# An adaLN block on one core: the FFN's modulation made as columns, and the first FFN input turned by VectorE and DMAs

## The chip, the cores and the metric

The kernel runs on one core of one Trainium2 chip. The metric is the device time of one execution in microseconds (us), the median over several runs. The engines are TensorE (PE, with its weight loads listed apart as PEld), VectorE (DVE), ScalarE (ACT) and GpSimd (POOL); SyncE (SP) issues most of the DMAs, ScalarE's queue a few.

## The reference

One transformer block with adaptive layer norm, batch B = 8, S = 1024 rows, D = 256, FFN width 1024, all in f32.

```python
mod = (silu(c) @ wmod).reshape(8, 6, 1, 256)          # c: 8x256, wmod: 256x1536
sa, ca, ga, sb, cb, gb = mod[:, 0..5]
ga = (2 * (ga >= 0) - 1) * maximum(abs(ga), 0.25)     # gb likewise
h = layernorm(x) * (1 + ca) + sa
scores = (h * w_lhs) @ (h * w_rhs).T                  # 1024 x 1024 per batch element
x = x + ga * (softmax(scores) @ h)
h = layernorm(x) * (1 + cb) + sb
x = x + gb * (relu(h @ W1 + b1) @ W2 + b2)
```

The six parts of mod are, in order, shift, scale and gate of the attention (0, 1, 2) and of the FFN (3, 4, 5).

## The kernel before

The batch elements b are worked through one after the other, in eight steps i of 128 rows each. A half g of a batch element is 512 rows, four tiles of 128. The FFN of batch element b - 1 (and of the first half of b) is done between the attention steps of b. The order of instructions on each engine is written out by hand: the last statement, `pin`, ties every instruction to the one before it on its engine, so an engine that waits holds up all that stands behind it. The same holds for the queue of SP.

**The scores** form a symmetric matrix (the two weightings meet in one product over d). For each tile of rows i `direct(b, i)` (L412) computes only from column tile i on, into PSUM tiles psc, and ScalarE copies them to sc. The rest of the column comes by mirroring: for b = 0 `mirror_first` turns 128x128 blocks on TensorE (ptm) and ScalarE copies them; for b > 0 `mirror` has VectorE turn 32x32 blocks (Tm, L435), and `move` writes them to DRAM in four DMAs (D_m, L306) and reads them back in another order in one (L309). `row_max(b, i)` (L463) takes the maximum of row tile i over all columns, and so needs the mirrors of the tiles before it. `max_turn` (pm, L468) turns the maximum on TensorE, `subtract` (L475) writes scores minus maximum to pT, `exponent` (L484) applies the exponential, and `product` (po, L501) multiplies by xg on TensorE. `product_out` (L513 and L515) divides, adds to x, and takes the statistics for the FFN's norm.

**Inputs of the FFN.** For half g, `ffn_rstd` makes the reciprocal deviation on ScalarE, `ffn_norm` the normalised rows xn in a tile X, `ffn_blocks` turns xn in 32x32 blocks on VectorE (T_f, L322) and sends it through DRAM with `move` (D_f, X_f), and `ffn_turn` applies the modulation modT into hT, VectorE for the first half of the columns and ScalarE for the other; POOL then makes the sums hs from hT. The first input, (0, 0), goes another way: its normalisation is on VectorE (L663) in step i = 6, and `ffn_turn`, in step i = 7, turns it with eight transposes on TensorE into PSUM (ptx, L695). `pair_products` (L726) of batch 1, step 0, is the first user of hT and hs.

**The modulation.** `mod_rows(part, parts)` (L194) computes parts of mod with the 8 batch elements on the partitions: scT, the silu of c, is the weight (8 columns) and up to 512 columns of wmod stream past; ScalarE copies the result to `mod`. `mod_columns(part)` (L210) turns two parts with four transposes so that d lies on the partitions. At the start mod_rows(0, 2) is made, then, once the second piece of wmod (wm) has landed, mod_rows(2, 1) and mod_rows(5, 1), just ahead of the first `direct`. VectorE then makes both gates at once and writes four rows for each batch element to rows_sb: two for the attention and two, gate and gate times b2, for the FFN. They go to DRAM as rows_d; `load_rows` reads the first two back for every batch element, and `load_last` the other two for the last one. mod_rows(3, 2) comes between mirror(0, 1) and max_turn(0, 1). In step i = 0 of batch 0, `make_columns` turns the two FFN rows into gcol (pt_g, L1031) and parts 3 and 4 into modT (pmc, L210, and L1073, L1074).

Of the kernel before, what the change touches and what calls it, by code (L numbers as in the profile page):

```python
# [17 lines left out]
P = 128  # L18
# [6 lines left out]
def adaln_block_kernel(  # L25
# [69 lines left out]
    c_sb, b2_row = early_d[:B, 0], early_d[:B, 1]  # L95
    wv, b1_rows = early_d[: 2 * ND, 2, 0:P], early_d[:NI, 3, 0:P]
# [18 lines left out]
    )  # L115
    load_x0(2, nc.sync)
# [3 lines left out]
    nc.sync.dma_start(out=b2_row, in_=b2.partition_broadcast(B))  # L120
# [9 lines left out]
    zeros, sign = early_a[:, 0], early_a[:B, 1].rearrange("b (j d) -> b j d", d=D)  # L130
    nc.vector.memset(zeros, 0.0)
    early_c = two.tile([P, 4, D], F32, tag="hT", name="early_c", bufs=1)
    rows_sb = early_c[:B]
# [39 lines left out]
    cols = const.tile([P, NI + 2 * ND], F32, name="cols")  # L173
# [7 lines left out]
    b1_col = lambda i: cols[:, i : i + 1]  # L181
    w_cols = lambda side: cols[:, ds(NI + side * ND, ND)].rearrange(
# [4 lines left out]
    mod, gate = early_b[:B, 0:6], early_b[:B, 6:8]  # L187
# [26 lines left out]


# [19 lines left out]
    def load_rows(b, queue=nc.scalar):  # L235
        queue.dma_start(out=rows_tile(b), in_=rows_d[b][0:2, :].partition_broadcast(P))
# [411 lines left out]
    def ffn_norm(b, g):  # L648
        mv, r = ffn.pop(("r", g))

        X = two.tile([P, NV, NT * V], F32, tag="X", name=f"X_f{b}_{g}", bufs=1)
        xn = X.rearrange("p a m -> p (a m)").rearrange("p (j d) -> p j d", d=D)
        if b + g > 0:
            shift = work.tile([P, TH], F32, tag="rs", name=f"rs_f{b}_{g}")
            nc.vector.scalar_tensor_tensor(shift, mv[:, :, 0], -1.0, r, ALU.mult, ALU.mult)
        for j in range(TH):
            if b + g > 0:
                nc.scalar.activation(
                    xn[:, j, :], x_t[b, g][:, j, :], AF.Identity,
                    scale=r[:, j : j + 1], bias=shift[:, j : j + 1],  # L660
                )
                continue
            nc.vector.tensor_scalar(  # L663
                xn[:, j, :], x_t[b, g][:, j, :], mv[:, j, 0:1], r[:, j : j + 1],
                ALU.subtract, ALU.mult,
            )
        ffn["xn", g] = xn, X
# [13 lines left out]
    def ffn_blocks(b, g):  # L681
        if (b, g) == (0, 0):
            return
        xn, X = ffn.pop(("xn", g))
        ffn["X", g] = turn_blocks(lambda k: xn[:, :, ts(k, P)], f"f{b}_{g}", X)

    def ffn_turn(b, g):
        hT = two.tile([P, ND, HALF], F32, tag="hT", name=f"hT_{b}_{g}", bufs=1)
        split = lambda T: T.rearrange("p (t a v) -> p t a v", a=NV, v=V)
        if (b, g) == (0, 0):  # L690
            xn, X = ffn.pop(("xn", g))[0], []
            for k in range(ND):
                pt = ps_t.tile([P, HALF], F32, tag="t", name=f"ptx_{b}_{g}_{k}")
                for t in range(TH):
                    nc.tensor.transpose(pt[:, ts(t, P)], xn[:, t, ts(k, P)], ident)  # L695
                X.append(split(pt))
        else:
            X = ffn.pop(("X", g))
            X = [X[:, k] for k in range(ND)]
        for k in range(ND):  # L700
            rows = split(hT[:, k, :])
            shift = modT[:, 0, k, b : b + 1]
            scale = modT[:, 1, k, b : b + 1]
            if k % 2 == 0:
                nc.vector.tensor_scalar(rows, X[k], scale, shift, ALU.mult, ALU.add)
            else:
                nc.scalar.activation(rows, X[k], AF.Identity, bias=shift, scale=scale)


        hs = two.tile([P, 3, H2], F32, tag="hs", name=f"hs_{b}_{g}", bufs=1)  # L710
        b11, b12 = hT[:, 0, 0:H2], hT[:, 0, H2:HALF]
        b21, b22 = hT[:, 1, 0:H2], hT[:, 1, H2:HALF]
        add = nc.gpsimd.tensor_tensor
        add(hs[:, 0], b12, b11, ALU.subtract)
        add(hs[:, 2], b22, b12, ALU.subtract)
        add(hs[:, 1], b22, hs[:, 0], ALU.subtract)
        add(b12, b21, hs[:, 1], ALU.subtract)
        ffn["hT", g] = hT, hs
# [170 lines left out]
    def load_last():  # L889
        last_ = two.tile([P, NT, NV, NT, V], F32, tag="sc", name="w2g", bufs=1)  # L890
        last_ = last_.rearrange("p i a j v -> p (i a j v)")
        w2g = last_[:, 0 : NI * D].rearrange("p (i d) -> p i d", d=D)
        rows = last_[:, NI * D : (NI + 2) * D].rearrange("p (j d) -> p j d", d=D)
        nc.sync.dma_start(out=w2g, in_=W2.rearrange("(k p) d -> p k d", p=P))
        nc.sync.dma_start(out=rows, in_=rows_d[B - 1][2:4, :].partition_broadcast(P))
        ffn["w2g"], ffn["grows"] = w2g, rows
        for i in range(NI):
            later(w2g[:, i, :], w2g[:, i, :], rows[:, 0, :], ALU.mult)
# [66 lines left out]
    def sum_weights():  # L965
# [16 lines left out]
    mod_rows(5, 1)  # L982
# [3 lines left out]


    raw = mod[:, 2:6:3, :]
    nc.vector.tensor_scalar(sign, raw, 0.0, 2.0, ALU.is_ge, ALU.mult)
    nc.vector.scalar_tensor_tensor(gate, raw, -1.0, raw, ALU.mult, ALU.max)  # L990
    nc.vector.tensor_scalar(gate, gate, GATE_MIN, None, ALU.max)
    nc.vector.scalar_tensor_tensor(gate, sign, -1.0, gate, ALU.add, ALU.mult)

    nc.vector.scalar_tensor_tensor(
        rows_sb[:, 0, :], mod[:, 1, :], 1.0, gate[:, 0, :], ALU.add, ALU.mult
    )
    nc.vector.tensor_tensor(rows_sb[:, 1, :], mod[:, 0, :], gate[:, 0, :], ALU.mult)
    nc.vector.tensor_copy(rows_sb[:, 2, :], gate[:, 1, :])
    nc.vector.tensor_tensor(rows_sb[:, 3, :], gate[:, 1, :], b2_row, ALU.mult)
# [5 lines left out]
    rows_d = dram.tile([B, 4, D], F32, name="rows_d")  # L1005
# [18 lines left out]

    gcol = const.tile([P, 2, ND, B], F32, name="gcol")

    def make_gcol():
        pg = ps_a.tile([P, HALF], F32, tag="a", name="pt_g")
        for j in range(2):
            for k in range(ND):  # L1030
                nc.tensor.transpose(  # L1031
                    pg[:, ts(j * ND + k, B)], rows_sb[:, 2 + j, ts(k, P)], ident[:B, :B]
                )
        nc.scalar.copy(gcol.rearrange("p j k b -> p (j k b)"), pg[:, : 2 * ND * B])
# [24 lines left out]
    mod_rows(3, 2)  # L1059
# [8 lines left out]
    def make_columns():  # L1068
        make_gcol()
        columns(b1_rows, 0)  # L1070
        nc.gpsimd.tensor_tensor(b1_step, cols[:, NH:NI], cols[:, 0:NH], ALU.subtract)
        pmb = mod_columns(3)
        nc.vector.tensor_copy(modT[:, 0], pmb[:, 0])  # L1073
        nc.vector.tensor_scalar(modT[:, 1], pmb[:, 1], 1.0, None, ALU.add)  # L1074

    def early(b, i):

        if b == 0:
# [3 lines left out]
            elif i == 5:  # L1082
                ffn_rstd(0, 0)
# [5 lines left out]
            elif i == 5:  # L1089
                prepare_turn(1, 0)  # L1090
            elif i == 6:
# [7 lines left out]
    def turns(b, i):  # L1099
# [6 lines left out]
        elif b == 0 and i == 3:  # L1106
            prepare_blocks(1, 1)
# [12 lines left out]
    def norms(b, i):  # L1120
# [18 lines left out]
        if i == 6:  # L1139
            if b == 0:  # L1140
                ffn_norm(b, 0)
# [8 lines left out]
    for b in range(B):  # L1150
        for i in range(NT):
# [8 lines left out]
            if (b, i) == (0, NT - 2):  # L1160

                prepare_turn(1, 1)
                product(b, i)
# [3 lines left out]
                mirror(*ahead)  # L1167
                early(b, i)
# [283 lines left out]
```

## Time and profile before

| | |
|---|---|
| time, median of 3 runs | 757.05 us (756.62 to 757.45) |
| the profiled execution, its own time | 756.93 us |
| its span in the trace | 755.1 us |
| PE busy | 749.1 us |
| PEld / DVE / ACT / POOL busy | 623.4 / 574.9 / 374.9 / 570.9 us |
| granted TensorE clock | full in all 40 slices |
| traffic with HBM | 50.62 MB read, 43.81 MB written |

Times in the profile are us from the start of the span. A row of the timeline has start and length of a group of like instructions, engine, line, operation, output<-input, and in brackets the idle time before it with what ended it. An f32 product on TensorE leaves two records, a transpose one. A row of the chain has start, length, engine, tile, line and the number of records. "SPq" rows are the issues of DMAs, not their transfers.

### The profile page before, as it was taken

The page shows a single profiled execution, that of the slowest core. Times are in us where ns is not written, and L with a number is a line of the kernel's source. Part 1 is how long each engine was busy: PE and PEld are TensorE (multiplying, and loading weights), DVE is VectorE, ACT ScalarE, POOL GpSimd, SP SyncE. Part 2 cuts the span into 40 slices and gives each one's busy share as a digit, 9 for nine tenths or more (in the row PEclk, how much of TensorE's full clock was granted, in tenths as well). Part 3 has the DMA queues.
Part 4 walks back from the last instruction along what each step waited for, and adds up shares of the span by engine and source line. Part 5 has one row for each costly group of instructions (what it writes and reads, how often), then busy time and mean ns, then how long its engine had stood idle before and what let it go on. Part 6 is the DMA issues. An engine that isn't in the chain of part 4 may idle for free.

```text
span 755.1 us, 11883 instructions
## 1 busy us (share of the span) xinstructions
PE 749.1 (99%) x3876; PEld 623.4 (83%) x3876; DVE 574.9 (76%) x1259; ACT 374.9 (50%) x688; POOL 570.9 (76%) x658
## 2 busy tenths in 40 slices
PE   8999999999999999999999999999999999999998
PEld 4686889788897888888888878988889788888887
DVE  7787879778796879968878688876889777685632
ACT  4554646635375454745546444563546535252521
POOL 3762796878968798788877699777996888669741
PEclk9999999999999999999999999999999999999999
DMA  9033442455443453445534555245553354133220
GB/s 308 16 112 98 131 133 74 135 178 152 127 120 123 153 153 110 147 118 158 164 99 119 153 154 161 74 127 172 155 152 85 119 166 133 50 91 126 84 85 28
DMA packets 106213, 95.21 MB, mean 126 GB/s; under 512 B 29700, under 2 KB 98848, under 8 KB 106152
## 3 DMA queue, kind: packets, MB, share of 16 engines
q1 hardware_dynamic: 98408, 85.81, 38.6%
q10 hardware_dynamic: 7744, 8.65, 3.7%
q8 instruction: 30, 0.49, 0.3%
q14 instruction: 31, 0.25, 0.1%
HBM read 50.62 MB, written 43.81 MB: 125 GB/s over the span
## 4 chain that ended last, share of the span: by engine, by line
PE 96%; DMA 1%; DVE 1%; ACT 1%; issue 0%
PE psc L412 16%; PE pa L726 11%; PE po L501 10%; PE pr L593 7%; PE pb L726 7%; PE pc L726 7%; PE yc L806 6%; PE ya L806 6%; PE yb L806 6%; PE pq L593 5%; PE pp L549 5%; PE py L916 4%; PE yd L806 3%; DMA wm<-in_L_wmod_dram 1%; PE pm L468 1%; PE pmr L194 0%
## 5 line engine op out<-in xcount | busy, mean ns | idle before, releaser
L412 PE MATMUL psc<-rT,lT 128*128 128x512 f32 (+3 forms) x384 | 134.8, 487 | 0.0
L780 POOL TENSOR_TENSOR f<-f,kept 128x512 f32<-128x512 f32 x64 | 81.5, 1274 | 42.8 <-DVE f L779 20.1
L419 ACT COPY sc<-psc 128x512 f32<-128x512 f32 (+3 forms) x96 | 44.7, 476 | 119.9 <-PE psc L412 113.0
L484 ACT ACTIVATE pT<-pT 128x1024 f32<-128x1024 f32 x64 | 67.6, 1056 | 70.6 <-DVE pT L475 70.5
L475 DVE TENSOR_TENSOR pT<-sc,pm 128x1024 f32<-128x1024 f32 x64 | 77.3, 1208 | 29.3 <-PE pm L468 13.7
L412 PEld LDWEIGHTS psc<-rT,lT 128*128 128x128 f32 x384 | 66.4, 191 | 37.2 <-issue 25.6
L501 PE MATMUL po<-xg,pT 128*128 128x257 f32 x352 | 80.6, 380 | 0.0
L463 DVE TENSOR_REDUCE m<-sc 128x1 f32<-128x1024 f32 x64 | 77.4, 1209 | 2.2 <-ACT sc L419 1.8
L501 PEld LDWEIGHTS po<-xg,pT 128*128 128x128 f32 x352 | 66.2, 190 | 10.0 <-issue 0.7
L747 ACT COPY kept<-pa 128x512 f32<-128x512 f32 x64 | 37.4, 584 | 69.3 <-PE pa L726 69.1
L726 PE MATMUL pb<-hs,w1s 128*128 128x256 f32 x256 | 65.9, 380 | 0.1
L726 PE MATMUL pc<-hT,w 128*128 128x256 f32 x256 | 65.7, 379 | 0.0
L880 POOL TENSOR_TENSOR x<-x,Y 128x512 f32<-128x512 f32 x28 | 35.1, 1276 | 29.3 <-DMA Y<-D_y 29.3
L789 ACT ACTIVATE f<-f 128x512 f32<-128x512 f32 x64 | 39.8, 622 | 34.7 <-POOL f L780 34.7
L642 POOL TENSOR_TENSOR x<-x,rows 128x256 f32<-128x256 f32 x64 | 44.8, 732 | 13.8 <-ACT rows L1022 10.6
L726 PEld LDWEIGHTS pb<-hs,w1s 128*128 128x128 f32 x256 | 48.5, 190 | 7.3 <-DVE f L765 0.8
L726 PEld LDWEIGHTS pc<-hT,w 128*128 128x128 f32 x256 | 48.6, 190 | 6.7
L806 PE MATMUL yc<-f,w2s 128*128 128x256 f32 x224 | 51.3, 379 | 0.0
L435 DVE STREAM_TRANSPOSE Tm<-sc 128x896 f32<-128x896 f32 (+6 forms) x49 | 34.3, 701 | 20.3 <-ACT sc L419 19.6
L806 PEld LDWEIGHTS yc<-f,w2s 128*128 128x128 f32 x224 | 41.5, 190 | 8.1 <-issue 2.9
L549 PEld LDWEIGHTS pp<-xg,pT 128*128 128x128 f32 x336 | 41.9, 192 | 5.1 <-DVE st_b L241 1.4
L799 POOL TENSOR_TENSOR ft<-f 128x256 f32<-128x256 f32 x56 | 40.8, 729 | 6.8 <-ACT f L790 6.8
(166 smaller groups left out, 1821.1 us busy)
## 6 DMA issues: line engine op xcount, KB each, us to landing
D_f<-T_f SPq DMA_DIRECT2D x60, 128.0 KB, 2.5
X_f<-D_f SPq DMA_DIRECT2D x15, 512.0 KB, 3.7
D_a<-T_a SPq DMA_DIRECT2D x56, 128.0 KB, 2.8
D_y<-T_y SPq DMA_DIRECT2D x56, 128.0 KB, 2.9
Y<-D_y SPq DMA_DIRECT2D x14, 512.0 KB, 3.4
out_dram<-x SPq DMA_DIRECT2D x14, 512.0 KB, 4.4
X_a<-D_a SPq DMA_DIRECT2D x13, 512.0 KB, 3.4
x<-in_L_attn_x_dram ACTq DMA_DIRECT2D x12, 512.0 KB, 3.4
```

The lines of the kernel that those rows point to most:

```text
L412: nc.tensor.matmul(psc[:, : hi - lo], lhsT=lT_t[b, i // TH][:, k, ts(i % TH, P)], rhs=rT_t[b, n][:, k, lo - n * HALF : HALF], start=(k == ...
L419: nc.scalar.copy(score_row(b, i)[:, lo // V : hi // V, :], psc[:, : hi - lo].rearrange("p (n v) -> p n v", v=V),)
L463: nc.vector.tensor_reduce(m, score_row(b, i), AX.XY, ALU.max)
L475: nc.vector.tensor_tensor(pT.rearrange("p j (a v) -> p j a v", v=V), score_columns(b, i), pm[:, :P].rearrange("p (j a v) -> p j a v", j=1, ...
L484: nc.scalar.activation(pT_t[b, i], pT_t[b, i], AF.Exp)
L501: nc.tensor.matmul(po[:, : D + 1], lhsT=pT[:, t, :], rhs=xg_t[b][:, t, 0 : D + 1], start=(t == 0), stop=(t == NT - 1),)
L549: nc.tensor.matmul(out, lhsT=lhs[:, t, :], rhs=xg_t[b][:, h * TH + t, P : P + XS], start=(t == 0), stop=(t == TH - 1),)
L593: nc.tensor.matmul(out, lhsT=lhs[:, t, :], rhs=rhs[:, t, :], start=(t == 0), stop=(t == TH - 1),)
L642: queue.append(lambda: nc.gpsimd.tensor_tensor(out, in0, row, op))
L726: nc.tensor.matmul(out, lhsT=lhsT, rhs=rhs, start=True, stop=True)
L780: nc.gpsimd.tensor_tensor(f[:, c::NH, hi], f[:, c::NH, hi], kept[:, None, hi].to_broadcast([P, 2, H2]), ALU.add,)
L806: nc.tensor.matmul(out, lhsT=lhs(c), rhs=rhs(c), start=(c == 0), stop=(c == NH - 1))
```

## The change

Parts 3, 4 and 5 of mod are no longer made as rows. A new function `mod_direct` takes 128x128 pieces of wmod as the weights and the 8 columns of scT as the moving operand: twelve products, whose result (128 partitions, 3 parts x 2 halves x 8 batch elements) ScalarE copies to mod_ffn. It stands where mod_rows(3, 2) stood; mod_rows(5, 1) and both sets of transposes in make_columns go. The FFN's gate, its product with b2 and modT are made from mod_ffn on VectorE (the four steps of the gate are now the function `make_gate`) in `keep_columns`, in step i = 6 of batch 0. b2 is loaded as two rows beside w_lhs and w_rhs, ahead of the second half of x's first element and of the second piece of wmod, and turned with them. rows_d keeps the two attention rows; for the last batch element two small DMAs write gcol's columns to last_d, from which load_last reads.

The first FFN input now goes like the others: `ffn_rstd(0, 0)` moves from step 5 to step 4, `ffn_norm(0, 0)` is on ScalarE in step 5 behind prepare_turn(1, 0), and `ffn_blocks(0, 0)` turns it on VectorE in step 6, behind prepare_turn(1, 1) and ahead of product(0, 6), and sends it through DRAM. The second half of batch 1's attention input, which held the tile X until now, gets the tile ft.

```diff
-    c_sb, b2_row = early_d[:B, 0], early_d[:B, 1]
-    wv, b1_rows = early_d[: 2 * ND, 2, 0:P], early_d[:NI, 3, 0:P]
+    c_sb = early_d[:B, 0]
+    wv, b1_rows = early_d[: 3 * ND, 2, 0:P], early_d[:NI, 3, 0:P]
...
+    nc.sync.dma_start(out=wv[2 * ND : 3 * ND, :], in_=b2.rearrange("(k p) -> k p", p=P))
     load_x0(2, nc.sync)
     load_x0(3, nc.sync)
     nc.sync.dma_start(out=wm[:, :, 2 * D : 6 * D], in_=wmod_v[:, :, 2 * D : 6 * D])
     nc.sync.dma_start(out=b1_rows, in_=b1.rearrange("(k p) -> k p", p=P))
-    nc.sync.dma_start(out=b2_row, in_=b2.partition_broadcast(B))
...
-    mod, gate = early_b[:B, 0:6], early_b[:B, 6:8]
+    mod, gate = early_b[:B, 0:3], early_b[:B, 6]
+    mod_ffn = early_c[:, 2, 0 : 3 * ND * B].rearrange("p (n k b) -> p n k b", n=3, k=ND)
+    MB = early_c[:, 3, 0 : 2 * ND * B].rearrange("p (n k b) -> p n k b", n=2, k=ND)
...
+    def mod_direct():
+        pc = ps_a.tile([P, HALF], F32, tag="a", name="pmd")
+        for n in range(3):
+            for h in range(ND):
+                for k in range(ND):
+                    nc.tensor.matmul(
+                        pc[:, ts(n * ND + h, B)],
+                        lhsT=wm[:, k, ds((3 + n) * D + h * P, P)],
+                        rhs=scT[:, k, :],
+                        start=(k == 0),
+                        stop=(k == ND - 1),
+                    )
+        nc.scalar.copy(
+            mod_ffn.rearrange("p n k b -> p (n k b)"), pc[:, : 3 * ND * B]
+        )
...
 def ffn_norm(b, g):
-        if b + g > 0:
-            shift = work.tile([P, TH], F32, tag="rs", name=f"rs_f{b}_{g}")
-            nc.vector.scalar_tensor_tensor(shift, mv[:, :, 0], -1.0, r, ALU.mult, ALU.mult)
+        shift = work.tile([P, TH], F32, tag="rs", name=f"rs_f{b}_{g}")
+        nc.vector.scalar_tensor_tensor(shift, mv[:, :, 0], -1.0, r, ALU.mult, ALU.mult)
         for j in range(TH):
-            if b + g > 0:
-                nc.scalar.activation(
...
-            nc.vector.tensor_scalar(
-                xn[:, j, :], x_t[b, g][:, j, :], mv[:, j, 0:1], r[:, j : j + 1],
-                ALU.subtract, ALU.mult,
+            nc.scalar.activation(
+                xn[:, j, :], x_t[b, g][:, j, :], AF.Identity,
+                scale=r[:, j : j + 1], bias=shift[:, j : j + 1],
             )
...
 def ffn_turn(b, g):
-        if (b, g) == (0, 0):
-            xn, X = ffn.pop(("xn", g))[0], []
-            for k in range(ND):
-                pt = ps_t.tile([P, HALF], F32, tag="t", name=f"ptx_{b}_{g}_{k}")
-                for t in range(TH):
-                    nc.tensor.transpose(pt[:, ts(t, P)], xn[:, t, ts(k, P)], ident)
-                X.append(split(pt))
...
+        X = ffn.pop(("X", g))
+        X = [X[:, k] for k in range(ND)]
...
     mod_rows(2, 1)
-    mod_rows(5, 1)
     direct(0, 0, range(1))
...
+    make_gate(gate, mod[:, 2, :], gate, sign)
...
-    rows_d = dram.tile([B, 4, D], F32, name="rows_d")
+    rows_d = dram.tile([B, 2, D], F32, name="rows_d")
...
     def make_gcol():
-        pg = ps_a.tile([P, HALF], F32, tag="a", name="pt_g")
-...
+        make_gate(gcol[:, 0], mod_ffn[:, 2], MB[:, 0], MB[:, 1])
+        nc.vector.tensor_tensor(gcol[:, 1], gcol[:, 0], w_cols(2), ALU.mult)
         for j in range(2):
+            nc.sync.dma_start(
+                out=last_d[j].rearrange("(k p) -> p k", p=P), in_=gcol[:, j, :, B - 1]
+            )
...
     exponent(0, 0)
-    mod_rows(3, 2)
+    mod_direct()
     max_turn(0, 1)
...
     def make_columns():
-        make_gcol()
         columns(b1_rows, 0)
         nc.gpsimd.tensor_tensor(b1_step, cols[:, NH:NI], cols[:, 0:NH], ALU.subtract)
-        pmb = mod_columns(3)
-        nc.vector.tensor_copy(modT[:, 0], pmb[:, 0])
-        nc.vector.tensor_scalar(modT[:, 1], pmb[:, 1], 1.0, None, ALU.add)
+
+    def keep_columns():
+        nc.vector.tensor_copy(modT[:, 0], mod_ffn[:, 0])
+        nc.vector.tensor_scalar(modT[:, 1], mod_ffn[:, 1], 1.0, None, ALU.add)
+        make_gcol()
...
-            elif i == 5:
+            elif i == 4:
                 ffn_rstd(0, 0)
...
             elif i == 5:
                 prepare_turn(1, 0)
+                ffn_norm(0, 0)
...
         elif b == 0 and i == 3:
-            prepare_blocks(1, 1)
+            X = two.tile([P, 3, NH, H2], F32, tag="ft", name="X_early", bufs=1)
+            X = X.rearrange("p j c r -> p (j c r)")[:, : ND * HALF]
+            prepare_blocks(1, 1, X.rearrange("p (b m) -> p b m", b=NV))
...
                 prepare_turn(1, 1)
+                ffn_blocks(0, 0)
                 product(b, i)
                 direct(*ahead)
                 exponent(*last_exponent)
                 product_out(b, i)
                 mirror(*ahead)
+                keep_columns()
                 early(b, i)
```

## The prediction

> **What bounds the kernel now.** I read the page first, then the chain that ended last for the first 130 us, then the timeline of 0 to 101 us and the SP queue's own. The page says that TensorE (PE) is the whole story:
>
> ```profile
> PE 749.1 (99%) x3876; PEld 623.4 (83%) x3876; DVE 574.9 (76%) x1259; ACT 374.9 (50%) x688; POOL 570.9 (76%) x658
> ...
> PE 96%; DMA 1%; DVE 1%; ACT 1%; issue 0%
> ```
>
> PE is busy for 749.1 of 755.1 us and carries 96% of the chain. So an edit counts by the PE time that it adds or removes, unless it makes PE wait. The change touches batch 0 and the start of batch 1 alone; the next view is the chain there (start, length, what):
>
> ```profile
> 11.11 1.89 PE pmr L194 x8
> ...
> 24.83 0.66 PE ptm L452 x6
> 25.48 1.81 PE pmr L194 x4
> 27.30 0.25 PE pm L468
> 27.55 1.75 PE po L501 x8
> ...
> 31.69 0.34 PE pt_g L1031 x4
> 32.09 0.25 PE pmc L210 x4
> ...
> 67.95 0.87 PE ptx L695 x8
> ...
> 110.20 0.90 PE pp L549 x8
> ```
>
> Here stands what is removed: half of the 11.11 piece (mod_rows(5, 1); the other half is mod_rows(2, 1)), the 25.48 piece (mod_rows(3, 2)), pt_g, pmc and ptx. An f32 product leaves two records, a transpose one. PE goes from piece to piece without a gap. The last view is the hand-over to batch 1, the SP queue and its consumers:
>
> ```profile
> 66.74 1.75 SPq L306 DMA_DIRECT2D D_m<-Tm  x4
> ...
> 70.26 0.61 SPq L309 DMA_DIRECT2D sc<-D_m  x1
> ...
> 70.92 2.09 SPq L306 DMA_DIRECT2D D_m<-Tm  x4
> ...
> 74.20 1.22 DVE L463 TENSOR_REDUCE m<-sc 128x1 f32<-128x1024 f32 x1 [0.43 <-DMA sc<-D_m]
> ...
> 76.70 0.48 DVE L762 SCALAR_TENSOR_TENSOR u<-pb,cols,kept 128x256 f32<-128x256 f32 x1 [1.29 <-PE pb L726]
> ...
> 78.42 1.21 DVE L475 TENSOR_TENSOR pT<-sc,pm 128x1024 f32<-128x1024 f32 x1
> ...
> 79.66 1.06 ACT L484 ACTIVATE pT<-pT 128x1024 f32<-128x1024 f32 x1 [0.17 <-DVE pT L475]
> ```
>
> Row_max(1, 1) (74.20) waits for the mirrored column that SP reads back at 70.26; behind it in VectorE's order stand pair_sums, the subtraction (78.42) and, on ScalarE, the exponent that ends at 80.72. PE begins product(1, 0) at 80.97: some 0.2 us of slack, plus the 1.29 us that VectorE idles before 76.70.
>
> **Part by part.** Five terms; minus is a gain.
>
> *mod_rows(5, 1) goes.* Four records of 256 columns; such records are spaced 0.216 us (four of pa take 0.86 in the chain), so 0.86 us of PE. Not all of it is gained: psc needs rT, whose second activation ends at 12.23, and the second half of lT, ready at 12.41. PE is free for it at 12.14 instead of 13.00; it starts near 12.35. Term -0.6, between -0.75 and -0.3, the poor end if b2's new DMA ahead of wm on SP (its neighbours took 0.26 and 0.31 us to issue) lands wm 0.3 us later. The gate chain on VectorE gets shorter (8x512 operations of 0.41 to 0.68 us become 8x256); it was ready at 16.46 for a PE step at 18.63, so that is worth nothing.
>
> *mod_direct for mod_rows(3, 2).* 3 x 2 x 2 = 12 products of 8 columns, 24 records, each with a full 128x128 load of weights, take the place of four records of 512 columns (4 x 0.43 = 1.72 us). No row has such a load under so few columns. The nearest below are the transposes of 8 rows: four pmc in 0.25, 0.062 each, 24 x 0.062 = 1.49. The nearest in kind are the f32 products of 128 columns, which also change weights at every record: pp 8 in 0.90, 0.112, so 2.69. The end above is a load that overlaps nothing: 190 ns by the page's PEld rows, 4.56. I take 0.112, since the load is the same and f32 loads show 190 ns against the transposes' 140. Term +0.97. Downwards it is capped: while mod_rows runs, the subtraction of row 0 (24.94 to 26.16) and the exponent (26.19 to 27.25) make the weights of po, which PE takes up at 27.30. A shorter mod_direct gains 0.15 at most. Bounds -0.15 and +2.84.
>
> The Trainium skill, "TensorE: Matmul & The Clock Gate", LDWEIGHTS, prices a load by its columns alone, 128/1.2 = 107 ns however few rows it has; the 62 ns of pmc, a 128-column load of 8 rows, contradict that for transposes, and no row settles it for f32. By that rule, as an estimate, mod_direct is 24 x 0.107 = 2.57 us: a rule against this edit.
>
> *pt_g and pmc(3) go from make_columns.* Eight transposes at 0.061: term -0.5, at most the pieces' 0.59. The small VectorE copies there move to 67 us.
>
> *ptx goes.* Eight transposes of 0.109: term -0.87. They lie between direct(1, 1) and product(0, 7), whose exponent ended at 66.52, so PE goes straight on.
>
> The four terms of PE: -0.6 + 0.97 - 0.5 - 0.87 = -1.0 us.
>
> *What replaces ptx, and the wait that it brings.* ffn_norm(0, 0) on ScalarE at i = 5: four activations (the like of L281 took 2.07 for four) between rT(1, 0) and rT(1, 1). The latter then ends near 62.5 instead of 60.8; psc uses it from 63.06 on. Hidden with 0.5 us to spare; were that gone, PE would lose the excess one for one. VectorE's two block transposes (1.29 for two, like T_a) come before product_out(0, 6), whose first step moves from 61.78 to about 63.4; its statistics are read at 76.25, so nothing waits. The seven gate steps and two of modT are 128x16 operations spaced 0.08 us (the four of sides): 0.8 us, in place of the four X_f steps of 1.34.
>
> The transfer is the point. SP runs in order: four writes of D_f, which start when the block transposes end, near 63.4; then the read of X_f, which waits for the writes to land; only then the mirror's four D_m writes that stood at 66.74; then its read, two new writes of last_d, and the next mirror. First write to read took 3.7 us on an idle queue (44.28 to 48.01) and up to 4.6 in company. So X_f's read is issued at 67.2 to 68.0 and D_m's writes start at 67.5 to 68.4, 0.8 to 1.7 late. They then run beside X_f's read, as later here:
>
> ```profile
> 91.20 0.34 SPq L309 DMA_DIRECT2D X_f<-D_f  x1
> 91.59 1.88 SPq L306 DMA_DIRECT2D D_m<-Tm  x4
> 96.03 0.53 SPq L309 DMA_DIRECT2D sc<-D_m  x1
> ```
>
> From write to read that is 4.4 us, against 3.5 at 66.74: 0.4 to 0.9 more. The mirrored column lands 1.2 to 2.5 us later, say 1.85. VectorE had 1.29 us of idle and PE about 0.2, together 1.5; but PE comes 0.87 earlier without ptx, which leaves 0.63. PE waits 1.85 - 0.63 = 1.2 us at product(1, 0); bounds 0 and 1.9. Term +1.2.
>
> X_f itself lands near 71.3; hT, then POOL's four steps of 0.73 end near 74.7, where PE's first use of the last of them, pc, is at 75.8. Hidden with 1 us. The last_d writes take SP about 0.8 us; 512 packets of 4 bytes are little (the trace's packets of 128 bytes took 13 ns: 0.4 us over 16 engines). The next mirror is read 2.6 us later and lands near 82, just ahead of row_max(1, 2) near 83; were that late, VectorE's 0.7 us of idle at 88.6 covers it first. The Trainium skill, "DMA: Bandwidth & Descriptors", Specifications, says that transfers under 512 B are done by read-modify-write; no packet here shows a price for that, and the sum has none.
>
> **Sum.** -1.0 + 1.2 = +0.2 us. The profiled execution took 756.93 us, 755.1 of span and 1.8 around it; so 757.1 for it, a span of 755.3. It lies 0.1 under the median of 757.05, so 757.2 by the median. About 0.2% (1.5 us) is what a measurement of this kernel can tell from no change.
>
> **Rivals.**
>
> *Faster: cheap loads and no wait.* If the 24 records run at the transposes' pace and the column lands in time, the terms are -0.75 - 0.15 - 0.59 - 0.87 = -2.4 at best; with ordinary startup and a small wait about -1.9: 755.2. For it: 128 columns did load in 62 ns. Against: f32 loads show 50 ns more, and SP's order leaves little hope of no wait. With loads at 0.112 and no wait it is -1.0, 756.0, inside the bound of no change. Chance of faster by over 0.2%: 0.24.
>
> *Slower: the queue decides.* The mechanism of the fifth term, in full: batch 2's load of x (512 KB, issued at 64.99 by ScalarE's queue), D_f, X_f and D_m collide, and row_max(1, 1) waits. Each us of landing beyond 0.63 goes to PE; from a delay of 3.1 us on it costs over 1.5 net. At 3.5: -1.0 + 2.9 = +1.9, 758.9. For it: three transfers now lie where one did. Against: the longest such write to read in this stretch is 4.6 us. Chance 0.17.
>
> *The direct product saves PE nothing.* Loads of 190 ns in a row: +1.87 on the sum, 759.1. For it: a record of 8 columns hides no load. Against: 62 ns for transposes shows that loads overlap the record before. Chance 0.11.
>
> **How the numbers follow.** The forecast, within 0.2%, has 0.48; faster 0.24; slower 0.17 + 0.11 = 0.28. The 8 in 10 range runs from 754.9, the cheap loads nearly in full, to 759.4, the serial loads with a little more wait.
>
> **What would show it.** Right: pmd's 24 records take about 2.7 us; psc starts near 12.35; no ptx; SP's D_m writes begin 1 us after the mirror's transpose; row_max(1, 1) waits over 1 us for sc<-D_m; PE shows a wait of about 1 us before product(1, 0). Wrong: PE without a gap at product(1, 0) and a span under 754; pmd over 4 us; or a new PE wait at psc L412 near 63 or at pa L726 near 74.

## The result and the profile after

| | before | after |
|---|---|---|
| median | 757.11 us, 5 runs (756.62 to 757.67) | 765.82 us, 5 runs (763.79 to 767.12) |
| ratio | | 1.0106 (1.0095 to 1.0117) |
| the profiled execution | 756.93 us | 765.82 us |

The change makes the kernel slower by 8.7 us, 1.1%, outside the range of the prediction. Its profiled execution has a span of 764.0 us. Two lines of the page after, the busy times and the chain's shares by engine:

```profile
PE 750.9 (98%) x3876; PEld 625.1 (82%) x3876; DVE 572.2 (75%) x1261; ACT 376.4 (49%) x690; POOL 571.0 (75%) x658
...
PE 90%; DMA 4%; DVE 3%; ACT 1%; issue 1%; SPq 1%; DVEq 0%
```

PE's busy time grew by 1.8 us and the span by 8.9. PE's share of the chain fell from 96% to 90%, and DMA's rose from 1% to 4%: PE waits now, and for transfers. The list of PE's waits over the first 130 us (what PE waited for: us in total, times, longest), its largest that the change can have made:

```profile
PE pa L730 <- ACT kept L751: 3.0, 1, 3.0
...
PE pmr L198 <- DMA wm<-in_L_wmod_dram: 1.2, 1, 1.2
PE pb L730 <- DVE f L769: 1.1, 1, 1.1
...
```

Three more of 0.5 to 0.6 us follow: pm for m, pb for POOL's hs, po for VectorE. Between 60 and 100 us before had no such wait. The timeline at the same places, PE's rows and VectorE's maxima:

```profile
12.07 1.03 PE L198 MATMUL pmr<-wm,scT 128*8 128x256 f32 x4 [1.20 <-DMA wm<-in_L_wmod_dram]
...
25.42 2.74 PE L225 MATMUL pmd<-scT,wm 128*128 128x8 f32 x24
...
72.90 0.55 DVE L709 TENSOR_SCALAR hT<-X_f,modT 128x512 f32<-128x512 f32 x1 [3.01 <-DMA X_f<-D_f]
...
77.95 1.22 DVE L484 TENSOR_REDUCE m<-sc 128x1 f32<-128x1024 f32 x1 [3.15 <-DMA sc<-D_m]
...
83.21 3.71 PE L522 MATMUL po<-xg,pT 128*128 128x257 f32 x16 [0.47 <-DVE rs_f L675]
...
91.00 1.22 DVE L484 TENSOR_REDUCE m<-sc 128x1 f32<-128x1024 f32 x1 [5.91 <-DMA sc<-D_m]
```

Row_max(1, 1) starts at 77.95 instead of 74.20, where the forecast looked for a wait; row_max(1, 2) at 91.00, after 5.91 us of idle. In before it had started at 82.64 without a wait, its column read back by SP at 75.39:

```profile
75.39 0.52 SPq L309 DMA_DIRECT2D sc<-D_m  x1
...
82.64 1.21 DVE L463 TENSOR_REDUCE m<-sc 128x1 f32<-128x1024 f32 x1
```

That second stall was not in the forecast. The SP queue of after shows both:

```profile
67.48 0.34 SPq L330 DMA_DIRECT2D X_f<-D_f  x1
67.87 1.93 SPq L327 DMA_DIRECT2D D_m<-Tm  x4
74.37 0.61 SPq L330 DMA_DIRECT2D sc<-D_m  x1
75.03 1.12 SPq L1036 DMA_DIRECT2D last_d<-gcol  x2
76.25 1.83 SPq L327 DMA_DIRECT2D D_m<-Tm  x4
86.90 0.53 SPq L330 DMA_DIRECT2D sc<-D_m  x1
```

The queue's read waits until the writes have landed, so the distance from the first write to the read tells how long the writes took. For the mirror behind X_f it is 6.5 us (67.87 to 74.37), where before had 3.5. For the mirror behind last_d it is 10.65 us (76.25 to 86.90), where before had 4.47 (70.92 to 75.39). The view of the DMAs for 62 to 95 us, in 40 slices of 0.83 us, says what the 16 DMA engines did in that time (busy tenths, then GB/s, then one row of the issues: KB each and median us from issue to landing):

```profile
DMA  0029968998980000299990905254310258930088
GB/s 0 0 56 211 267 145 313 314 248 243 326 275 35 24 7 0 39 278 263 208 143 0 4 0 5 7 9 16 42 43 0 11 153 300 304 107 0 1 173 281
...
D_m<-Tm SPq DMA_DIRECT2D x4, 96.0 KB, 9.2
```

From 81.8 to 86.7 us they are one to five tenths busy and move 5 to 43 GB/s; a slice of six tenths at 66.1 us moved 145. In the slice from 80.2 us they are nine tenths busy and move 4 GB/s. So the engines are occupied with little. The four writes of 96 KB take 9.2 us to land; in the same view of before they took 3.0:

```profile
D_m<-Tm SPq DMA_DIRECT2D x4, 96.0 KB, 3.0
```

The chain has the same two transfers, and leads from them over row_max(1, 2) to PE's pa at 95.62:

```profile
77.65 9.17 DMA D_m<-Tm
...
86.90 4.08 DMA sc<-D_m
```

Behind that stall comes a third loss. Two rows of the table by windows (us, busy time of PE, PEld, DVE, ACT, POOL, then PEclk, DMA share, GB/s):

```profile
95.00:99.00 4.00, 3.38 (x9) 2.73 (x10) 3.90 (x10) 1.15 (x3) 0.42 (x1) 0.62 0.68 187
```

```profile
95.95:99.36 3.41, 3.41 (x10) 2.69 (x9) 3.38 (x7) 0.58 (x1) 0.78 (x1) 0.50 0.57 167
```

The granted clock, full in all of before's slices, is 0.62 on average over these four microseconds. The second row resolves it: the clock is exactly half for 3.41 us and full on both sides. In that stretch records of 256 columns are 0.43 us apart instead of 0.216, so a stretch under a busy PE costs about 1.7 us.

### The profile page after: what moved, and what is told of

Same layout as the page of the kernel before. It is cut to its first block, busy times and chain, and to the rows that moved or that the text cites. A ratio compares the mean times of both kernels' runs of the same rounds, so it can differ in the third digit from the quotient of the medians.

```text
span 764.0 us, 11903 instructions
## 1 busy us (share of the span) xinstructions
PE 750.9 (98%) x3876; PEld 625.1 (82%) x3876; DVE 572.2 (75%) x1261; ACT 376.4 (49%) x690; POOL 571.0 (75%) x658
## 4 chain that ended last, share of the span: by engine, by line
PE 90%; DMA 4%; DVE 3%; ACT 1%; issue 1%; SPq 1%; DVEq 0%
PE psc L433 16%; PE pa L730 10%; PE po L522 9%; PE pr L614 7%; PE pb L730 6%; PE yc L810 6%; PE pc L730 6%; PE ya L810 6%; PE yb L810 6%; PE pq L614 5%; PE pp L570 5%; PE py L920 4%; PE yd L810 3%; DMA D_m<-Tm 1%; DMA wm<-in_L_wmod_dram 1%; PE pm L489 1%
```

## The experiments

Four theories stand in the expectations. L: the many 4-byte runs of last_d hold up the mirror's writes behind them on SP's queue. Q: X_f's place ahead of the mirror on SP's queue does it all. S: b2's early DMA makes wm land late. G: mod_direct, in one piece, takes the clock down. The kernel before ran beside each set, at 757.14 to 757.33 us in the median (beside i1 to i3 once, 757.14).

A yardstick serves all of them: the start of three PE steps in the profiled execution (product(0, 7), product(1, 0), and the first pp of batch 1), and the time from the first D_m write of mirror(1, 1) to its read. Up to product(0, 7) before, e2, e3, f4, h3 and i1 to i3 have the same instructions and still differ by 0.76 us there (68.20 to 68.96), so the distances between the steps say more than the starts.

| kernel | product(0, 7) | product(1, 0) | pp | mirror(1, 1), write to read | median, us | ratio |
|---|---|---|---|---|---|---|
| before | 68.66 | 80.97 | 92.76 | 4.47 | 757.1 to 757.3 | |
| after | 68.04 | 83.21 | 100.87 | 10.65 | 765.82 | 1.0106 (1.0095 to 1.0117) |
| e1_last_early | 73.33 | 88.59 | 100.45 | 4.39 | 764.25 | 1.0095 (1.008 to 1.011) |
| e2_before_short_runs | 68.64 | 80.95 | 94.28 | 10.02 | 759.84 | 1.0035 (1.0025 to 1.0046) |
| e3_before_long_runs | 68.96 | 83.00 | 94.78 | 3.7 | 758.58 | 1.0021 (1.0011 to 1.003) |
| e4_input_alone | 67.83 | 83.66 | 95.52 | 4.60 | 759.29 | 1.0026 (1.0016 to 1.0036) |
| f1_b2_late | 68.81 | 84.15 | 100.68 | 9.89 | 764.25 | 1.0097 (1.0079 to 1.0115) |
| f2_b2_late_rows | 67.06 | 82.39 | 94.25 | 4.57 | 759.22 | 1.004 (1.0029 to 1.0051) |
| f3_all_moved | 69.57 | 82.08 | 93.94 | 4.47 | 757.71 | 1.000 (0.9991 to 1.0009) |
| f4_before_long_runs2 | 68.20 | 80.52 | 92.30 | 3.67 | 756.75 | 0.9992 (0.9983 to 1.0001) |
| h1_input_moved | 67.93 | 80.24 | 92.06 | 4.47 | 756.42 | 0.9989 (0.998 to 0.9998) |
| h2_direct_split | 67.76 | 80.25 | 92.11 | 4.51 | 756.52 | 0.9989 (0.998 to 0.9998) |
| h3_before_half_the_runs | 68.75 | 81.06 | 94.57 | 10.72 | 759.51 | 1.0036 (1.0024 to 1.0049) |
| i1_runs_apart | 68.55 | 80.87 | 92.65 | 3.74 | 758.87, one run | |
| i2_few_runs | 68.55 | 80.86 | 92.65 | 5.03 | 758.08, one run | |
| i3_runs_of_64 | 68.25 | 80.56 | 92.35 | 3.85 | 756.70, one run | |

### e1_last_early: the changed kernel, with last_d written in step 0

```diff
                 mirror(*ahead)
-                keep_columns()
...
                     make_columns()
+                    keep_columns()
```

> The changed kernel with keep_columns moved from step 6 to the end of step 0 of batch 0, where SP's queue is empty until 44 us; the two last_d DMAs go with it. Theory L (the 512 four-byte runs of last_d hold up the mirror behind them): the mirror of row 1 goes from write to read in about 4.5 us instead of 10.7, the waits at 91.7 and 92.6 us and the half clock behind them go, some 6 us: 759 to 760 us. Theory Q (the X_f transfer ahead of the mirror on SP does it all, last_d is innocent): at least 764 us.

The mirror answers for L: from write to read 4.4 us instead of 10.65, and from product(1, 0) to pp 11.86 us instead of 17.66 (before: 11.79). The total does not fall as L said, since this execution lost as much elsewhere. It is 5.3 us behind after at product(0, 7): wm came later still (PE idle 1.82 us) and the clock was half for 3.41 us behind that wait (from 12.70 us) and once more from 29.76 us, so that it was 0.60 on average from 30 to 34 us, with PE busy for all 4.00 us. Two small VectorE steps of the gate took 1.13 and 1.20 us, where after had 0.17 and 0.18 for them. So the second stall goes with last_d's place, and the total says nothing on its price.

### e2, e3 and f4: the same DMAs in the kernel before

e2 adds to the kernel before what the change adds to SP, and nothing else (last_d is not read):

```diff
+    last_d = dram.tile([2, D], F32, name="last_d")
...
                 mirror(*ahead)
+                for j in range(2):
+                    nc.sync.dma_start(
+                        out=last_d[j].rearrange("(k p) -> p k", p=P), in_=gcol[:, j, :, B - 1]
+                    )
                 early(b, i)
```

> The kernel before, with two added DMAs that write 2 x 256 values of gcol to a DRAM tile in runs of 4 bytes, behind the mirror of row 0 of batch 1 in SP's order; nothing reads them. Theory L: they alone cost 3 to 6 us, 760 to 763, and the mirror of row 1 takes about 10 us from write to read (4.5 without). Theory Q: under 0.5 us, 757.0 to 757.6.

e3 writes the same 2 KB as two runs of 1 KB from rows_sb:

```diff
+                    nc.sync.dma_start(
+                        out=last_d[j : j + 1, :], in_=rows_sb[B - 1 : B, 2 + j, :]
+                    )
```

> As the run with short runs, but the same 2 KB of data leave as two DMAs of one 1 KB run each (row 7 of rows_sb), in the same place. If the length of the runs is what costs, this is the time of the kernel before within 0.5 us, 756.6 to 757.6; if any two more DMAs in this place cost (their issue of about 0.5 us each, their completion), it shows like the short runs do, 760 or more.

e2's SP queue, with the same stall as after, in a kernel that has nothing else of the change:

```profile
70.86 1.12 SPq L1170 DMA_DIRECT2D last_d<-gcol  x2
72.09 1.84 SPq L306 DMA_DIRECT2D D_m<-Tm  x4
82.11 0.53 SPq L309 DMA_DIRECT2D sc<-D_m  x1
```

It costs 2.6 us in the median, a little under the 3 to 6 that L gave it. The mirror takes 5.5 us longer, and in the profiled execution PE waits 1.3 us for it at a full clock. e3's mirror was not held up (3.7 us), but the kernel was 1.4 us slower than before all the same, which neither theory forecast. Its trace shows why: rows_sb lies in early_c, whose memory hT takes next, so hT waited for the DMA, and the chain has 2.52 us of last_d<-early_c. f4 takes the source from w1 and is the clean pair to e2:

```diff
+                    nc.sync.dma_start(out=last_d[j : j + 1, :], in_=w1[j : j + 1, 0, 0:D])
```

> The kernel before with two added DMAs of one 1 KB run each, read from w1, which nothing writes any more at that time, in the place of the short runs of the earlier run. If the length of the runs costs, the time of the kernel before, within 0.5 us; the mirror of row 1 takes 4 to 5 us from write to read. If any two DMAs in that place cost, 1.4 us or more as with the rows of rows_sb.

Two DMAs of as many bytes, at the same place on the queue (70.44), leave the mirror its 3.67 us (71.30 to 74.97) and cost nothing that can be measured: 0.9992 (0.9983 to 1.0001). It is the form of the writes, not their number on SP or their 2 KB.

### e4_input_alone and h1_input_moved: X_f's place on the queue

e4 is the kernel before with the FFN input's half of the change alone; mod's parts stay as rows, last_d and mod_direct are absent:

```diff
-            elif i == 5:
+            elif i == 4:
                 ffn_rstd(0, 0)
...
                 prepare_turn(1, 0)
+                ffn_norm(0, 0)
...
                 prepare_turn(1, 1)
+                ffn_blocks(0, 0)
                 product(b, i)
```

> The kernel before with the second half of the change alone: the first FFN input normalised on ScalarE, turned by VectorE and sent through DRAM; mod and gcol as before, no last_d. Theory L with Q's share: PE saves 0.87 us of transposes and waits 2.9 us up to product(1, 0) as in the changed kernel, 758.5 to 759.5. Theory Q alone: about the whole loss, 763 or more. As I had summed it before: 757.4.

```profile
67.34 0.34 SPq L309 DMA_DIRECT2D X_f<-D_f  x1
67.72 1.92 SPq L306 DMA_DIRECT2D D_m<-Tm  x4
74.24 0.61 SPq L309 DMA_DIRECT2D sc<-D_m  x1
```

It has the 6.5 us, and PE loses 3.5 us between product(0, 7) and product(1, 0): 15.83 us against before's 12.31. From there to pp it loses nothing more (11.86). So Q is right for the first stall, and cannot be the second. h1 has the same half with its steps moved earlier, so that D_f and X_f are through before the mirror comes; against e4:

```diff
             elif i == 4:
-                ffn_rstd(0, 0)
+                ffn_norm(0, 0, range(2))
...
             elif i == 5:
                 prepare_turn(1, 0)
-                ffn_norm(0, 0)
+                ffn_blocks(0, 0)
...
+        elif b == 0 and i == 4:
+            ffn_rstd(0, 0)
+        elif b == 0 and i == 5:
+            ffn_norm(0, 0, range(2, TH))
...
                 prepare_turn(1, 1)
-                ffn_blocks(0, 0)
                 product(b, i)
```

> The kernel before with the FFN input's half of the change alone, mod as before, and the normalisation in steps 4 and 5, the turn in step 5. If the transfer ahead of the mirror was the whole cost of that half, PE keeps the 0.87 us of transposes and waits for nothing: 756.2 us, and the clock is full in all executions. Theory G (mod_direct, 2.7 us of 8-column products, lets the clock gate halve the clock in some executions) expects no execution at a mean clock of 0.998 or less here.

```profile
63.51 0.34 SPq L309 DMA_DIRECT2D X_f<-D_f  x1
66.88 1.86 SPq L306 DMA_DIRECT2D D_m<-Tm  x4
70.92 0.61 SPq L309 DMA_DIRECT2D sc<-D_m  x1
```

The mirror's writes begin 3.4 us behind X_f's read instead of 0.4, and take 4.0 us. Product(1, 0) follows product(0, 7) after 12.31 us, as in before, and PE waits for nothing between 60 and 100 us. The median is 756.42 us, 2.9 less than e4 and 0.9 less than before beside it; the forecast was 756.2. None of its 11 executions has a mean clock under 0.999, as G said of a kernel without mod_direct.

### f1, f2 and f3: repairs of the changed kernel, one upon the other

f1 loads b2 beside b1, behind wm:

```diff
-    nc.sync.dma_start(out=wv[2 * ND : 3 * ND, :], in_=b2.rearrange("(k p) -> k p", p=P))
...
+    nc.sync.dma_start(out=b1_rows[NI : NI + ND, :], in_=b2.rearrange("(k p) -> k p", p=P))
```

> The changed kernel with b2's rows loaded behind wm and b1 on SP and turned with b1, not ahead of x's second half and wm. Theory S (b2's early DMA lands wm about 1 us later): wm lands near 11.1 to 11.5 us instead of 12.0 to 12.4, psc starts near 12.4 instead of 13.0 to 14.0, and the kernel gains about 0.7 us or, where the longer wait halved the clock, 2 to 3: 763 to 765 us. Rival: wm lands when it lands, no change, 764 to 766.

wm came in time for a wait of 0.4 us instead of 1.2, and the first product of scores started 0.9 us earlier (12.12 against 13.03). S is right about the wait. But the total, 764.25 us, has an interval that overlaps after's, and its profile says why the gain cannot be seen. The rows by windows, and PE's rows in them:

```profile
26.00:30.00 4.00, 4.00 (x19) 3.48 (x19) 2.22 (x2) 0.64 (x2) 3.92 (x5) 0.62 0.01 2
```

```profile
23.59:27.00 3.41, 3.41 (x31) 3.25 (x30) 1.22 (x1) 2.46 (x4) 3.41 (x6) 1.00 0.00 0
27.00:30.41 3.41, 3.41 (x11) 2.82 (x11) 2.63 (x3) 0.20 (x1) 3.33 (x4) 0.50 0.01 2
```

```profile
24.51 2.85 PE L225 MATMUL pmd<-scT,wm 128*128 128x8 f32 x24
...
27.46 3.36 PE L522 MATMUL po<-xg,pT 128*128 128x257 f32 x8
```

Right behind mod_direct the clock is half for 3.41 us, with PE busy throughout, and the eight records of product(0, 0) take 3.36 us; in after they took 1.90 (from 28.16 on). Even so f1 meets after at pp (100.68 against 100.87): both wait there for the same late mirror, which ate the difference.

f2 is f1 with last_d written as rows: one transpose of gcol's four columns on TensorE, a copy, and one DMA of four runs of 512 B at the end of step 7:

```diff
-        for j in range(2):
-            nc.sync.dma_start(
-                out=last_d[j].rearrange("(k p) -> p k", p=P), in_=gcol[:, j, :, B - 1]
-            )
...
+        nc.tensor.transpose(
+            pv[: 2 * ND, :P], gcol[:, :, :, B - 1].rearrange("p j k -> p (j k)"), ident
+        )
+        nc.scalar.copy(last_rows_t, pv[: 2 * ND, :P])
+        nc.sync.dma_start(
+            out=last_d.rearrange("j (k p) -> (j k) p", p=P), in_=last_rows_t
+        )
```

> As the run with b2 late, and the last batch's gate columns are turned by one transpose on TensorE at the end of step 7 of batch 0 and leave as one DMA of four 512-byte runs, behind the mirror of row 1, instead of 512 four-byte runs ahead of it. Theory L: the mirror of row 1 takes 4 to 5 us from write to read, no wait over 1 us past 85 us, 758.5 to 760. Theory Q (the order on SP alone): 763 or more.

The mirror takes 4.57 us, product(1, 0) to pp 11.86, and the total falls by 5.0 us to 759.22. That is what the short runs at their place cost in the changed kernel, though the medians mix executions with a different number of half-clock stretches. Like with like, f1's two at a mean clock of 0.998 (763.14 and 763.24) against f2's six at 0.999 or more (median 759.1) give 4.1, and the others of both give about 4.5. Some 1.7 of that is the half-clock stretch behind the stall, which e2's profiled execution did not have. f2 changes the form and the place of the DMA at once: it now stands behind mirror(1, 1), and the next mirror, behind it, takes 5.08 us where before had 4.82. That the form alone decides is f4's result.

f3 is f2 with h1's move of the input:

```diff
-                ffn_norm(0, 0)
+                ffn_blocks(0, 0)
...
                 prepare_turn(1, 1)
-                ffn_blocks(0, 0)
                 product(b, i)
```

> As the last, and the first FFN input is normalised on ScalarE in steps 4 and 5 and turned in step 5 behind prepare_turn(1, 0), so that X_f's transfer is over before the mirror of row 0 is written. If the rest of the loss is that transfer ahead of the mirror, no wait of PE is left between 60 and 100 us and the four PE terms of the prediction remain: -0.6 + 0.97 - 0.5 - 0.87 = -1.0, 756.0 to 756.5. If it lies elsewhere in the new way of the input (ScalarE, VectorE, hT), it stays at 758.5 or more.

No PE wait is left between 60 and 100 us; the median is 757.71. Its eleven executions part by their mean granted clock: five at 0.999 to 1.0 took 755.99 to 757.11 us, six at 0.997 to 0.998 took 757.71 to 758.76. The profiled one is of the second kind, and the table by windows shows where the clock fell; from 30 to 34 us, the next row, it is 0.75. The half-clock stretch is again 3.41 us long (28.61 to 32.02):

```profile
26.00:30.00 4.00, 4.00 (x26) 3.61 (x27) 1.83 (x3) 1.36 (x3) 3.92 (x6) 0.83 0.01 2
```

### h2_direct_split: mod_direct in two pieces

f3 with 16 of the 24 records in place and the last 8, for the gate, in make_columns:

```diff
-    mod_direct()
+    mod_direct(range(2))
     max_turn(0, 1)
...
     def make_columns():
+        mod_direct(range(2, 3))
```

> The run with all moved, with mod_direct in two pieces: parts 3 and 4 where it stood (16 records, 1.8 us, as long as the rows that it replaced), part 5 in make_columns (8 records, 0.9 us). Theory G: no low stretch is as long as before, so the executions with a mean clock of 0.997 go, and the median comes to that of the undisturbed ones, 755.6 to 756.4. If the clock falls for another reason (the start, chance), about half of the executions stay at 757.7 to 758.8.

```profile
30.00:34.00 4.00, 4.00 (x23) 3.13 (x22) 3.71 (x12) 1.75 (x6) 3.84 (x4) 1.00 0.00 0
```

All 11 executions had a mean clock of 0.999 or more, and the median is 756.52, 1.2 under f3 and 0.1 above the forecast's range. The amount of work is the same. That supports G: with 24 records in one piece the clock falls in about half of the executions, at some 1.7 us each (the medians of the two groups, 756.4 and 758.1), and with 16 and 8 it did not. f3 and h2 ran on different chips, but e1's profile, on the chip of h2, also has the fall behind the one piece.

The profiles say more on why it is only about half. The recorded clock changes only at whole multiples of 3.413 us behind the start of its first full stretch, and that start differs from execution to execution (5.0 to 8.1 us). So mod_direct lies differently on this grid each time. Where the clock fell behind it, its records had 2.35 (e1), 2.49 (f1, from 24.51 to 27.00) and 2.60 us (f3) of the 3.41 us just before; where it stayed full, at most 2.26 (after, from 25.42 to 27.68), 1.56 (f2) and, split, 1.53 (h2). These six profiles fit a limit between 2.26 and 2.35 us, but no run varied it on purpose, and what the clock responds to is not shown.

### h3 and i1 to i3: what it is about the short runs

Each is the kernel before with one DMA of a given form at e2's place, into a last_d that nothing reads. h3 is e2 with one of its two DMAs, 256 runs of 4 bytes:

```diff
+                for j in range(1):
```

> The kernel before with one of the two DMAs of 4-byte runs (256 runs, not 512) in the same place. If the runs are paid one by one, the mirror of row 1 takes from write to read about halfway between 4.5 us (none) and 10.0 us (512), some 7 us, and the time is within 1 us of before since row_max(1, 2) then waits little: 757 to 758. If it is a fixed price of such a DMA, 10 us again.

i1 writes 256 runs of 4 bytes that lie 512 B apart:

```diff
+    last_d = dram.tile([ND, P, P], F32, name="last_d")
...
+                nc.sync.dma_start(
+                    out=last_d[:, :, 0].rearrange("k p -> p k"), in_=gcol[:, 0, :, B - 1]
+                )
```

> The kernel before with one added DMA of 256 runs of 4 bytes in the same place, each run to an address 512 bytes from the next. If writes of 4 bytes to neighbouring bytes of DRAM get in each other's way, the mirror of row 1 is back to 4 to 6 us from write to read; if each short write costs wherever it goes, 10 us again.

i2 writes 32 runs of 4 bytes, neighbours in two groups of 16:

```diff
+                nc.sync.dma_start(
+                    out=last_d[0].rearrange("(k p) -> p k", p=P)[0:16], in_=gcol[0:16, 0, :, B - 1]
+                )
```

> The same with 32 runs of 4 bytes to neighbouring addresses (16 partitions, 2 values each). If the delay grows with the number of neighbouring runs up to some limit, 4.5 to 6 us from write to read; if one such DMA has a fixed price, 10 us.

i3 writes 128 runs of 64 B side by side:

```diff
+    last_d = dram.tile([P, ND * B], F32, name="last_d")
...
+                nc.sync.dma_start(out=last_d, in_=gcol[:, 0].rearrange("p k b -> p (k b)"))
```

> The same with 128 runs of 64 bytes to neighbouring addresses. If runs of 4 bytes are the trouble for sharing a line of DRAM, 4.5 to 5 us from write to read; if any run below 512 bytes is, about 10 us.

SP's rows of i1:

```profile
70.97 0.61 SPq L1169 DMA_DIRECT2D last_d<-gcol  x1
71.68 1.89 SPq L306 DMA_DIRECT2D D_m<-Tm  x4
75.42 0.53 SPq L309 DMA_DIRECT2D sc<-D_m  x1
```

h3's own rows:

```profile
71.06 0.61 SPq L1170 DMA_DIRECT2D last_d<-gcol  x1
71.78 1.87 SPq L306 DMA_DIRECT2D D_m<-Tm  x4
82.50 0.53 SPq L309 DMA_DIRECT2D sc<-D_m  x1
```

The same number of runs, of the same four bytes, from the same tile, differ in their distance in DRAM, and the wait behind them falls from 10.72 to 3.74 us. 64-byte neighbours cost nothing (3.85). 32 neighbours of 4 bytes cost 0.6 us against before (5.03 against 4.47) or 1.4 against f4, which also has a DMA in that place (3.67). 256 cost as much as 512. So neither the length of a run nor its count decides by itself, but many small writes to bytes that lie side by side. Each form was seen in one profile, distances between 4 and 512 B were not tried, and how the memory serialises the writes is not seen in any row. h3's delay did not halve, and its total, 759.51, is near e2's. i1's total, 758.87 in its one execution, is not explained by the queue: it starts pp 0.1 us earlier than before. Single executions of before beside the other sets ran from 756.31 to 759.20.

## Why the prediction was wrong

Its own steps, in its order, read from the profiled execution of after:

| step | predicted | measured |
|---|---|---|
| mod_rows(5, 1) goes | -0.6 | +0.1 |
| mod_direct for mod_rows(3, 2) | 2.69 us, net +0.97 | 2.74 us, net +0.67 |
| pt_g and pmc go | -0.5 | -0.51 |
| ptx goes | -0.87 | -0.88 |
| the wait at product(1, 0) | +1.2 | +2.86 |
| last_d | 0 | +5.9 up to pp |
| sum up to pp | +0.2 | +8.1 |

**The step that failed is the sixth row, last_d, to which the sum gave nothing.** The prediction priced last_d at 0.8 us on SP and 0.4 us of packets, hidden, and put the next mirror's read 2.6 us later; it came 11.5 us later (86.90 against 75.39). The issue took 1.12 us; the packets of 4 bytes even show a median of 9 ns each. The price is in the writes behind them, whose landing went from 3.0 to 9.2 us: single packets of theirs took up to 6.8 us in the trace, in before none over 0.04. VectorE's 0.7 us of idle could not cover that: row_max(1, 2) came 8.4 us late and PE waited 3.6 us for it (0.6 at pm, 3.0 at pa). Counted from start to start, against the same pieces of before, pm came 0.8 us later behind pc and pa 3.2 later behind pm, and at the half clock the ten records from 95.62 to 99.57 took 3.95 us instead of 2.15, 1.8 more. That makes 5.8 of 5.9. f1 to f2 put it at 4 to 5 us in the total, and e2 alone showed the same stall in the kernel before.

The prediction drew here on the Trainium skill, "DMA: Bandwidth & Descriptors", Specifications, on read-modify-write below 512 B, and gave it no price because no packet showed one. Trace and rule meet halfway: writes of 4 bytes were the cost, but 64-byte runs and 4-byte runs 512 B apart are also below that size, and behind them the mirror took 3.85 and 3.74 us. A price should have been set as a bound from above, since no row of before showed a write of that form.

**The fifth term was right in kind and too small.** SP's order and its times came out within 0.3 us: D_f at 63.44, X_f's read at 67.48, D_m's writes at 67.87. The size of the delay failed. The prediction took 4.4 us from write to read, from a later place where X_f and D_m run together; here it was 6.5. The load of x(2, 0) still ran when X_f's read came, and D_m's packets began only at 70.3 us, while X_f's ran from 68.5 to 72.4. X_f itself landed at 72.8, not 71.3, so the 1 us of cover for hT and POOL's sums was gone, and PE waited 0.56 for hs. The column was 3.75 us late and PE lost 2.86. That is the rival "the queue decides" almost to the figure: for a delay of 3.5 us it gave a wait of 2.9 and 758.9 us. e4, where only this was at work, took 759.29. After's 765.82 needed the second stall as well. What the load of x(2, 0) added was not tried by itself: in h1 it still runs beside D_m, and the mirror takes 4.0 us.

**The first term.** The prediction saw that b2's new DMA stands ahead of wm and allowed for 0.3 us. wm's issue came 0.5 us later (4.12 against 3.64), and the product that needs it started at 12.07, not 11.11; the 0.6 us were gone. f1 shows that the place of that DMA did it, though not what it was worth in the end. With b2 late the first product of scores starts at 12.05 to 12.87 (f2, f1, h2, f3), against 12.93 in before and 13.08 in h1. That is a gain of 0.1 to 0.9 us, with the term of 0.6 inside, spread by when wm and rT come.

**mod_direct was priced right**, at 0.112 us a record. The estimate of 2.57 us by the Trainium skill, "TensorE: Matmul & The Clock Gate", LDWEIGHTS, is near the measured 2.74 as well. The 62 ns of the transposes were the wrong neighbour. What no step had is the clock. Before was at full clock in all slices, so the prediction had no row for a change of it. After's own profile kept it through mod_direct; those of e1, f1 and f3 did not.

The two rivals that were about mod_direct's pace fell with its 2.74 us. The net of the modulation's half, -0.13 by the prediction (-0.6 + 0.97 - 0.5), can't be told from nothing: h2 reaches product(0, 7) 0.17 us ahead of h1, which lacks that half, but equal instructions differ by up to 0.76 us there, and their totals, 756.52 and 756.42, are the same. So the modulation's half has shown no gain. h1, the input's half alone with its steps moved ahead, drops ptx and has no wait of PE between 60 and 100 us; it measured 0.9989 of before, with an interval that just excludes no change (0.998 to 0.9998). f4, which only adds two DMAs to before, measured 0.9992, so a gain of 0.1% is not secured by this.

In the totals the way back reads: after 765.82; b2 late, 764.25 (within the intervals, the same); last_d as rows, 759.22; input moved ahead, 757.71; mod_direct split, 756.52; before 757.1 to 757.3.

## What to carry to other kernels

Price a small DMA by what stands behind it in its queue too, not only by its own bytes or its packets' times. Here it helped to turn a column into a row on TensorE before it was written to DRAM, and to put it where nothing was awaited. Where a transfer is put ahead of one that is just in time, the delay of the second is a term of its own; moving the first one step earlier was worth 2.9 us here. When two stalls follow each other, repairing one alone can show nothing, since the later one takes up what the first gives back, so repair them one upon the other and read the stages in between. And a clock that differs between executions mixes into medians: compare executions at the same mean clock.

## What the runs showed of the hardware that was not expected

- 256 writes of 4 bytes to neighbouring addresses delayed the landing of the next DMA by about 6 us (10.72 against 4.47); 512 B apart they did not (3.74).
- Each fall of the granted clock ahead of the last product of these profiles is to one half, for 3.41 us (after, e1, f1, f3); 0.62 or 0.75 are averages over a longer window. The Trainium skill, "TensorE: Matmul & The Clock Gate", Part 1, ties half rate to an idle window of about 3.4 us. The length agrees. But in the 3.41 us just before a fall PE was busy for 0.39 us behind the stall in after, for 1.48 behind the wait for wm in e1, and for all 3.41 around mod_direct in e1, f1 and f3. So a PE that the profile shows as busy did not keep its clock.
- The two gate steps of 128x16 in e1 took 1.13 and 1.20 us, with POOL busy for 3.44 of the 4 us around, and 0.17 and 0.18 in after, where POOL was idle from 65 to 69 us. The two end at 40.11 and 41.35, each 0.03 to 0.04 us behind the end of a POOL operation of 1.3 us, which points to POOL. But others of the same shape in e1 took 0.16 in the same company, so the cause stays open.
